# First Q ahead of K, V's first load behind its stores, and the last block's VectorE steps in source order

## The chip, the core and the metric

The kernel runs on one core of a Trainium2 chip. A core has five engines that run side by side and meet at semaphores: TensorE (PE in the profile, with PEld for its weight loads), VectorE (DVE), ScalarE (ACT), GpSimd (POOL) and SyncE (SP). Here SP does nothing but issue DMA transfers, in order: an issue that has to wait holds everything behind it. Each of the other engines works through its own instructions in order as well. The metric is the device time of one execution, in microseconds; lower is better.

## The reference

One transformer layer in float32 on x of shape (4, 2048, 256): attention with 16 heads of size 16 over 2048 keys, a layer norm, a gated feed-forward net of width 704 whose activations and weights are rounded blockwise (16 elements) to a 4-bit float grid, and a second layer norm.

```python
q, k, v = (split_heads(x @ W.T) for W in (Wq, Wk, Wv))      # 16 heads of 16
attn = softmax(einsum('bhld,bhmd->bhlm', q, k) / 4, axis=-1)
o = merge_heads(einsum('bhlm,bhmd->bhld', attn, v)) @ Wo.T
x = layernorm(x + o)
h = silu(fp4_linear(x, w_gate)) * fp4_linear(x, w_up)
x = layernorm(x + fp4_linear(h, w_down))                     # fp4_linear rounds both operands
```

## The kernel before

**Tiles and steps.** The queries are cut in blocks of 512 (`QB`), the keys in tiles of 128, the heads in four groups of four (`NG`, `HG`). A step is one group of heads for one query block: 4 x 4 x 4 = 64 steps of 16 key tiles. Each key tile is one period of the main loop (lines 860 to 898). In a period the maxima of a later key tile run ahead (`maxima`, 20 periods ahead: `LEAD`), the exponentials of the present one follow (`exponentials`), and two periods behind (`LAG`) the products with V (`values`). `period` fills each period with one or two parts of other work: projections of later blocks, the feed-forward net of finished ones, and the preparation of its weights (`prepare`).

**The start.** Lines 232 to 242 issue the first loads: x on SP's queue, the weights of K, Q and V on ScalarE's. `turn_w` transposes K's and then Q's weights. The loop at line 846 then projects the first 512 rows for K and Q, heads 0 to 7 ("k0", "q0"), and rows 512 to 2047 for K alone. `project` (line 333) transposes x, multiplies, splits each product into a high part (`hi`, ScalarE) and a rest (`lo`, GpSimd), and stores both to DRAM tensors `kx` and `qx`, four stores for each (line 362). `load_k` and `load_q` fetch them back per head: four transfers of 64 rows for K, four of 62 rows for Q. Only then can the first `maxima` run, which need both. V's projections are filled into the first 12 periods (m = 0 to 11 in the loop, n = m - 20); each stores to `vx` (line 378). V's first load is issued at n == 0 (line 867), in the period in which the exponentials begin.

**The end.** After the last period nothing but the last query block's own tail is left. `feed_forward_last` (line 678) does it in four tiles of 128 rows, t = 0 to 3, out of these pieces:

- `attended(t)`: output projection `py` on TensorE, added to x1 on VectorE (line 709), then `moments(t)`: two statistics steps on VectorE, two steps on GpSimd for the inverse deviation `rstd`;
- `quantized(t)`: normalises (line 699) and rounds to the 4-bit grid (`fp4_at_once`): 11 VectorE steps that each read the one before;
- `up(t)`: two transposes `ptq`, copied by ScalarE, then products `pg` and `pu`, read by ScalarE;
- `hidden(t)`: the gate's product and its rounding, 14 VectorE steps on 352 or 704 columns;
- `downward(t)`: transposes `pth`, copied by ScalarE, then the product `pz`;
- `added(t)` and `stored(t)`: adding `pz` (line 769), second layer norm, store to `out`.

**What sets the order.** A tile framework schedules what the source records. Matrix products are kept in the source's order (`matmul` and `transpose`, lines 134 to 138, call `keep_in_program_order`). For the other engines the framework picks among what it holds to be ready; in the last block it interleaves the VectorE steps of different tiles.

Of the kernel before, what the change touches and what calls it, by code (L numbers as in the profile page):

```python
# [35 lines left out]
ALU = mybir.AluOpType  # L36
# [34 lines left out]
    return 0 if j % 2 == 0 else DH  # L71


@with_exitstack
def block_kernel(
    ctx: ExitStack,
# [9 lines left out]
    out: bass.AP,  # L86
):
    nc = tc.nc
    B, L, D = x.shape
    FF = w_gate.shape[0]  # L90
    KC = D // P
    NQB = L // QB
# [75 lines left out]

    def fp4_at_once(pool, t, tag, gain=1.0):

        step = nc.vector
        p, nb, _ = t.shape
        amax = pool.tile([p, nb], F32, tag="amax" + tag, name="amax")
        step.tensor_reduce(amax, t, AX.X, ALU.max, apply_absolute_value=True)
        sc = pool.tile([p, nb], F32, tag="sc" + tag, name="sc")
        step.tensor_scalar(sc, amax, gain / 6.0, 1e-12, ALU.mult, ALU.max)
        rs = pool.tile([p, nb], F32, tag="rs" + tag, name="rs")
        step.reciprocal(rs, sc)
        step.tensor_scalar(rs, rs, gain * TIES_DOWN, 1.0, ALU.mult, ALU.mult)
        xn = pool.tile([p, nb, FB], F32, tag="xn" + tag, name="xn", bufs=3 if tag else 2)  # L180
        step.tensor_tensor(xn, t, rs.unsqueeze(2).to_broadcast([p, nb, FB]), ALU.mult)
        m = pool.tile([p, nb, FB], F32, tag="m" + tag, name="m", bufs=1)
        step.tensor_single_scalar(m.bitcast(I32), xn.bitcast(I32), EXPONENT, ALU.bitwise_and)
        step.tensor_scalar(m, m, 1.0, ROUND, ALU.max, ALU.mult)
        step.tensor_tensor(xn, xn, m, ALU.add)
        step.tensor_tensor(xn, xn, m, ALU.subtract)
        step.tensor_tensor(xn, xn, sc.unsqueeze(2).to_broadcast([p, nb, FB]), ALU.mult)
        return xn
# [27 lines left out]
    def load_x(b, tb):  # L216

        rows = slice(tb * QB, (tb + 1) * QB)
        if b == 0 and tb >= 2:
            xb_of[b, tb] = p1.tile([P, QT, D], F32, tag="x1", name="xb", bufs=2)  # L220
        else:
            xb_of[b, tb] = p2.tile([P, QT, D], F32, tag="xb", name="xb")
        nc.sync.dma_start(xb_of[b, tb], x[b, rows, :].rearrange("(t p) d -> p t d", p=P))
# [6 lines left out]
        nc.scalar.dma_start(loaded[name], w.rearrange("(c p) k -> p c k", p=P))  # L230

    load_x(0, 0)
    load_w("wk", wk)
    load_w("wq", wq)
    for tb in range(1, NQB):
        load_x(0, tb)
    ones = p2.tile([P, 2 * NC * L // P], F32, tag="a", name="ones")
# [6 lines left out]
    def turn_w(name, dst):  # L244
        for kc in range(KC):
# [7 lines left out]
            for n in range(KC):  # L253
# [2 lines left out]
                    pt[:, n * P : (n + 1) * P].rearrange("p (h d) -> p d h", h=NC),  # L256
                )

    turn_w("wk", wkT)
    turn_w("wq", wqT)  # L260


    RF = FF // 8
# [414 lines left out]
    def feed_forward_last(b, qb, x1):  # L678

        heads = [oTs[(b * NQB + qb) * KC + c] for c in range(KC)]  # L680
        xqT = p1.tile([P, KC, QB], F32, tag="xqT", name="xqT")
        xq, gates, hq, hT, norms = {}, {}, {}, {}, {}

        def wide(name):
            return p1.tile([P, QB], F32, tag="e", name=name, bufs=E_BUFS)

        def moments(t):
            st = p2.tile([P, 6], F32, tag="st", name="st")
            nc.vector.bn_stats(st, x1[:, t, :])
            mv = p2.tile([P, 4, 2], F32, tag="mv", name="mv")  # L690
            nc.vector.bn_aggr(mv[:, 0, :], st)
            rstd = p2.tile([P, 2], F32, tag="rstd", name="rstd")
            nc.gpsimd.tensor_scalar_add(rstd[:, :1], mv[:, 0, 1:2], LN_EPS)
            nc.gpsimd.tensor_tensor(rstd[:, :1], rstd[:, :1], minus_half[:, :1], ALU.pow)
            norms[t] = mv, rstd

        def normed(t):
            mv, rstd = norms.pop(t)
            nc.vector.tensor_scalar(
                x1[:, t, :], x1[:, t, :], mv[:, 0, 0:1], rstd[:, :1], ALU.subtract, ALU.mult  # L700
            )

        def attended(t):
            py = psum("py")
            for c in range(KC):
                matmul(
                    py[:, :D], heads[c][:, t * P : (t + 1) * P], woT[:, c, :], start=(c == 0), stop=(c == KC - 1)
                )
            nc.vector.tensor_add(x1[:, t, :], x1[:, t, :], py[:, :D])
            moments(t)  # L710

        def quantized(t):
            normed(t)
            xq[t] = fp4_at_once(p2, x1[:, t].rearrange("p (b f) -> p b f", f=FB), "")

        def up(t):
            pt = psum("ptq")[:, : KC * P].rearrange("p (k n) -> p k n", k=KC)
            for kc in range(KC):
                transpose(pt[:, kc, :], xq[t].rearrange("p b f -> p (b f)")[:, kc * P : (kc + 1) * P], ident)
            nc.scalar.copy(xqT[:, :, t * P : (t + 1) * P], pt)  # L720
            gates[t] = []
            for half in range(2):
                cols = slice(half * FH, (half + 1) * FH)
                pg, pu = psum("pg"), psum("pu")
                for bank, w in ((pg, wgT), (pu, wuT)):
                    for kc in range(KC):
                        matmul(
                            bank[:, :FH],
                            xqT[:, kc, t * P : (t + 1) * P],
                            w[:, kc, cols],  # L730
                            start=(kc == 0),
                            stop=(kc == KC - 1),
                        )
                a, g, u = (wide(name)[:, :FH] for name in "agu")
                nc.scalar.activation(a, pg[:, :FH], AF.Tanh, scale=0.5)
                nc.scalar.copy(g, pg[:, :FH])
                nc.scalar.copy(u, pu[:, :FH])
                gates[t].append((a, g, u))

        def hidden(t):  # L740
            h = p2.tile([P, FF], F32, tag="h", name="h")
            for half, (a, g, u) in enumerate(gates.pop(t)):
                nc.vector.scalar_tensor_tensor(a, a, 1.0, g, ALU.add, ALU.mult)
                nc.vector.tensor_mul(h[:, half * FH : (half + 1) * FH], a, u)
            hq[t] = fp4_at_once(p2, h.rearrange("p (b f) -> p b f", f=FB), "h", gain=0.5)

        def downward(t):
            if t % 2 == 0:
                hT[t // 2] = p2.tile([P, 2, NFC, P], F32, tag="hT", name="hT", bufs=1)
            q, dst = hq[t].rearrange("p b f -> p (b f)"), hT[t // 2][:, t % 2]  # L750
            for c0 in range(0, NFC, 4):
                pt = psum("pth")
                for c in range(c0, min(c0 + 4, NFC)):
                    w = min(P, FF - c * P)
                    transpose(pt[:w, (c - c0) * P : (c - c0 + 1) * P], q[:, c * P : c * P + w], ident)
                if c0 == 0:
                    nc.scalar.copy(dst[:, :4, :].rearrange("p c n -> p (c n)"), pt)  # L757
                    continue
                for c in range(c0, NFC):
                    w = min(P, FF - c * P)  # L760
                    nc.scalar.copy(dst[:w, c, :], pt[:w, (c - c0) * P : (c - c0 + 1) * P])
            pz = psum("pz")
            for c in range(NFC):
                w = min(P, FF - c * P)
                matmul(pz[:, :D], dst[:w, c, :], wdT[:w, c, :], start=(c == 0), stop=(c == NFC - 1))
            return pz

        def added(t, pz):
            nc.vector.tensor_add(x1[:, t, :], x1[:, t, :], pz[:, :D])
            moments(t)  # L770

        def stored(t):
            normed(t)
            at = qb * QB + t * P
            nc.sync.dma_start(out[b, at : at + P, :], x1[:, t, :])

        attended(0)
        attended(1)
        quantized(0)
        up(0)  # L780
        attended(2)
        quantized(1)
        up(1)
        hidden(0)
        attended(3)
        quantized(2)
        pz = downward(0)
        up(2)
        hidden(1)
        added(0, pz)  # L790
        quantized(3)
        pz = downward(1)
        up(3)
        hidden(2)
        stored(0)
        added(1, pz)
        pz = downward(2)
        hidden(3)
        stored(1)
        added(2, pz)  # L800
        pz = downward(3)
        stored(2)
        added(3, pz)
        stored(3)
# [39 lines left out]


    for tb in range(NQB):
        for _ in projection(0, tb, ("k0", "q0") if tb == 0 else ("k0",)):
            pass
        load_k(0, tb)
        if tb == 0:  # L850
            load_q(0)
    turn_w("wv", wvT)
    for tb in range(NQB):
        queue.append(projection(0, tb, ("v",)))
# [5 lines left out]
    for n in range(-LEAD, N + LAG):  # L860
        m = n + LEAD
        (sm, im), (s, kt), (sv, kv) = divmod(m, NKT), divmod(n, NKT), divmod(n - LAG, NKT)
        if m in (8, 10, 12, 14):
            if m == 8:
                load_q(1)
            load_k(1, m // 2 - 4)
        if n == 0:
            load_v(0)
        if n == N - NKT:
            x1_last = load_last(*steps[-1][:2])  # L870
# [64 lines left out]
```

## Time and profile before

| What | Value |
|---|---|
| median of 3 runs | 3654.88 us (3651.22 to 3658.14) |
| the profiled execution, as timed | 3651.45 us |
| its span, from first to last instruction | 3649.4 us |
| TensorE busy | 3534.1 us, 97% of the span |
| VectorE, ScalarE, GpSimd busy | 77%, 74%, 34% |
| mean granted TensorE clock | 0.989 |
| first score product | 27.40 us |
| first product with V | 99.19 us |
| last product with V, then the last block's tail | ends at 3572.1 us; the tail takes some 77 us |

The profile gives for each instruction its start, its duration, its source line and shape, and in square brackets how long its engine had stood idle before it and what ended that wait. A "chain" line tells on which engine the time that set the end was spent. In the rows of SP the duration is that of issuing a transfer, not of the transfer. TensorE is busy nearly all of the span; the exceptions lie in the first slice and the last one of the forty into which the page cuts the span.

### The profile page before, as it was taken

What the parts mean: (1) busy time and instruction counts of PE and PEld (TensorE: products, weight loads), DVE (VectorE), ACT (ScalarE), POOL (GpSimd) and SP (SyncE); (2) the same over time, 40 slices, a digit from 0 to 9 for tenths busy, and PEclk for the clock granted to TensorE, in tenths of its full rate; (3) what the DMA queues carried; (4) which work ended last, traced back from release to release, by engine and by line L of the source; (5) the groups of instructions that cost most, each with busy time, mean ns of one, the idle gap of its engine ahead of it and who ended that gap; (6) DMA issues with size and microseconds to landing.
All of it is one profiled execution on the core that took longest, in us unless ns stands there. A gap on an engine that the chain in (4) does not pass through costs nothing.

```text
span 3649.4 us, 57772 instructions
## 1 busy us (share of the span) xinstructions
PE 3534.1 (97%) x21348; PEld 1593.8 (44%) x21348; DVE 2816.2 (77%) x3310; ACT 2691.0 (74%) x5446; POOL 1251.3 (34%) x1496
## 2 busy tenths in 40 slices
PE   7889999999999999999999999999999999999996
PEld 5333444444444444444444444444443434444343
DVE  5777778787787778778787787878778787888845
ACT  3677777777777777777777777777777777777772
POOL 1331423434243242424324243342424325142430
PEclk9999999999999999999999999999999999999998
DMA  6533323323232322323223232322322221222100
GB/s 219 164 123 99 119 68 113 89 85 103 82 98 87 105 84 83 116 68 116 85 85 106 80 100 86 97 85 83 109 69 77 67 84 50 86 66 81 57 21 6
DMA packets 190640, 328.39 MB, mean 90 GB/s; under 512 B 24344, under 2 KB 68248, under 8 KB 190360
## 3 DMA queue, kind: packets, MB, share of 16 engines
q1 hardware_dynamic: 188968, 323.39, 29.1%
q8 instruction: 171, 2.80, 0.3%
q10 hardware_dynamic: 1392, 1.31, 0.1%
q14 instruction: 109, 0.89, 0.1%
HBM read 237.04 MB, written 86.51 MB: 89 GB/s over the span
## 4 chain that ended last, share of the span: by engine, by line
PE 82%; DVE 12%; DMA 2%; POOL 2%; issue 1%; ACT 1%; SPq 0%; POOLq 0%; ACTq 0%; DVEq 0%
PE av L135 24%; PE pe L135 18%; PE pm L135 16%; DVE mx L432 9%; PE pz L135 6%; PE pg L135 5%; PE pu L135 5%; PE pq L135 3%; PE pv L135 2%; PE pth L138 1%; PE pa L138 1%; PE py L135 1%; PE pn L138 1%; DMA qx<-qhi 1%; DVE st L524 1%
## 5 line engine op out<-in xcount | busy, mean ns | idle before, releaser
L432 DVE TENSOR_REDUCE mx<-pm 128x2 f32<-128x1024 f32 x2048 | 2408.6, 1217 | 666.5 <-PE pm L135 662.2
L466 ACT ACTIVATE e<-pe 128x512 f32<-128x512 f32 x4096 | 2218.8, 596 | 676.0 <-PE pe L135 670.8
L135 PE MATMUL av<-e,v 128*32 128x512 f32 x8192 | 1098.0, 608 | 4.2 <-DMA v<-vx 4.2
L135 PE MATMUL pe<-q,k 64*128 64x512 f32 x4096 | 1036.4, 456 | 4.9 <-ACT e L466 4.5
L135 PEld LDWEIGHTS pe<-q,k 64*128 64x128 f32 x4096 | 476.6, 184 | 968.5 <-ACT e L466 853.8
L135 PE MATMUL pm<-k,q 62*128 62x512 f32 x4096 | 805.1, 448 | 67.1 <-DVE mx L432 57.5
L135 PEld LDWEIGHTS pm<-k,q 62*128 62x128 f32 x4096 | 346.8, 185 | 382.7 <-DVE mx L432 178.2
L135 PEld LDWEIGHTS av<-e,v 128*32 128x32 f32 x8192 | 162.1, 108 | 335.5 <-issue 312.9
L572 POOL TENSOR_TENSOR a<-a,g 128x352 f32<-128x352 f32 x120 | 112.6, 938 | 494.5 <-ACT a L571 494.5
L135 PE MATMUL pz<-wdT,hT 128*128 128x128 f32 (+1 forms) x1488 | 233.4, 299 | 1.5 <-ACT hT L757 1.5
L617 POOL TENSOR_TENSOR x<-x,read 128x128 f32<-128x128 f32 x120 | 54.8, 456 | 482.2 <-ACT read L143 482.2
L135 PEld LDWEIGHTS pz<-wdT,hT 128*128 128x128 f32 x1488 | 190.5, 193 | 50.5 <-ACT e L466 18.2
L163 POOL TENSOR_TENSOR xn<-xn,m 128x704 f32<-128x704 f32 (+2 forms) x100 | 153.6, 1536 | 153.5 <-DVE m L162 131.6
L586 POOL TENSOR_TENSOR h<-a,u 128x352 f32<-128x352 f32 x120 | 112.4, 937 | 226.0 <-ACT u L585 224.0
L135 PE MATMUL pg<-wgT,xqT 128*128 128x352 f32 x512 | 186.5, 487 | 1.9 <-ACT xqT L720 1.9
L135 PE MATMUL pu<-wuT,xqT 128*128 128x352 f32 x512 | 185.0, 484 | 0.0
L548 POOL TENSOR_TENSOR x<-x,read 128x256 f32<-128x256 f32 x60 | 43.8, 730 | 374.0 <-ACT read L143 374.0
L164 POOL TENSOR_TENSOR xn<-xn,m 128x704 f32<-128x704 f32 (+2 forms) x100 | 153.8, 1538 | 5.4
L165 POOL TENSOR_TENSOR xn<-xn,sc 128x704 f32<-128x704 f32 (+2 forms) x100 | 126.4, 1264 | 7.5
L573 POOL TENSOR_TENSOR a<-a,g 128x352 f32<-128x352 f32 x120 | 113.9, 949 | 9.4
L135 PEld LDWEIGHTS pg<-wgT,xqT 128*128 128x128 f32 x512 | 87.5, 190 | 60.2 <-ACT e L466 19.1
L135 PEld LDWEIGHTS pu<-wuT,xqT 128*128 128x128 f32 x512 | 87.6, 189 | 58.1 <-ACT e L466 20.0
(114 smaller groups left out, 2278.8 us busy)
## 6 DMA issues: line engine op xcount, KB each, us to landing
k<-kx SPq DMA_DIRECT2D x1024, 128.0 KB
v<-vx SPq DMA_DIRECT2D x64, 768.0 KB
q<-qx SPq DMA_DIRECT2D x256, 124.0 KB
kx<-khi SPq DMA_DIRECT2D x64, 256.0 KB
qx<-qhi SPq DMA_DIRECT2D x64, 256.0 KB
vx<-vt SPq DMA_DIRECT2D x32, 384.0 KB
xb<-in_L_attn_x_dram SPq DMA_DIRECT2D x16, 512.0 KB
kx<-klo SPq DMA_DIRECT2D x32, 256.0 KB
```

Source lines behind the costliest of these rows:

```text
L135: tc.keep_in_program_order(nc.tensor.matmul(*args, **kw))
L138: tc.keep_in_program_order(nc.tensor.transpose(*args))
L163: nc.gpsimd.tensor_tensor(xn, xn, m, ALU.add)
L164: nc.gpsimd.tensor_tensor(xn, xn, m, ALU.subtract)
L165: nc.gpsimd.tensor_tensor(xn, xn, sc.unsqueeze(2).to_broadcast([p, nb, FB]), ALU.mult)
L432: nc.vector.tensor_reduce(mx_sb[s][:, t, 2 * i : 2 * i + 2, kb], pm, AX.X, ALU.max)
L466: nc.scalar.activation(e, pe[j], AF.Exp, scale=SCALE)
L548: nc.gpsimd.tensor_add(x1[:, t, :], x1[:, t, :], read(py[:, :D]))
L572: nc.gpsimd.tensor_mul(a, a, g)
L573: nc.gpsimd.tensor_add(a, a, g)
L586: nc.gpsimd.tensor_mul(h[:, cols], a, u)
L617: nc.gpsimd.tensor_add(x1[:, t, cols], x1[:, t, cols], read(pz))
```

## The change

Three things change.

1. At the start Q goes before K: its weights are loaded and transposed first, the first projection makes Q before K (so Q's four stores are issued before K's), and `load_q(0)` stands before `load_k(0, 0)`.
2. V's first load is no longer tied to n == 0. It is issued in the first period in which all of V's projections are recorded, which is m = 12 (n = -8).
3. In the last block VectorE's steps go through a wrapper, `InOrder`, that keeps them in the source's order; and `hidden(0)` is moved behind `attended(3)` and `quantized(2)`.

```diff
+class InOrder:
+    def __init__(self, tc, engine):
+        self.tc, self.engine = tc, engine
+
+    def __getattr__(self, name):
+        return lambda *args, **kw: self.tc.keep_in_program_order(getattr(self.engine, name)(*args, **kw))
...
+    vector = InOrder(tc, nc.vector)
...
     load_x(0, 0)
+    load_w("wq", wq)
     load_w("wk", wk)
-    load_w("wq", wq)
...
+    turn_w("wq", wqT)
     turn_w("wk", wkT)
-    turn_w("wq", wqT)
...
-            nc.vector.tensor_add(x1[:, t, :], x1[:, t, :], py[:, :D])
+            vector.tensor_add(x1[:, t, :], x1[:, t, :], py[:, :D])
...
         attended(2)
         quantized(1)
         up(1)
-        hidden(0)
         attended(3)
         quantized(2)
+        hidden(0)
         pz = downward(0)
         up(2)
         hidden(1)
...
-        for _ in projection(0, tb, ("k0", "q0") if tb == 0 else ("k0",)):
+        for _ in projection(0, tb, ("q0", "k0") if tb == 0 else ("k0",)):
             pass
-        load_k(0, tb)
         if tb == 0:
             load_q(0)
+        load_k(0, tb)
...
-        if n == 0:
+        if 0 not in v_sb and all((0, tb, "v") in projected for tb in range(NQB)):
             load_v(0)
```

The other replacements of `nc.vector` by `vector` are of the same kind: in `fp4_at_once`, `moments`, `normed`, `hidden` and `added`, which the last block alone uses.

In the two built programs every engine's instructions stand in the same order but for four places. Q and K are swapped at the start on all engines. SP's queue has V's first load among the K loads of the second step, four K loads after the last `vx` store and ahead of K's stores for heads 8 to 15. On VectorE the first reduction of `prepare` (`amax` on `wl`, line 150) stands one `mx` reduction later. And VectorE's last block runs in this order, where before the steps of neighbouring pieces alternated:

```
after:  add0 add1 | norm0+round0 | add2 | norm1+round1 | add3 | norm2+round2
        | hidden0 | hidden1 | added0 | norm3+round3 | hidden2
        | norm(stored0) added1 | hidden3 | norm(stored1) added2
        | norm(stored2) added3 | norm(stored3)
before: round0 and round1 alternate, ahead of add2; hidden0 alternates with
        add2, norm2+round2 and hidden1; hidden1 with added0 and round3; and so on
```

TensorE's order in the last block is the same in both: `py0 py1 ptq0 up(0) py2 ptq1 up(1) py3 pth0 pz0 ptq2 up(2) pth1 pz1 ptq3 up(3) pth2 pz2 pth3 pz3`.

More of the change, by code (lines that the diff above doesn't have):

```diff
@@ L169, in fp4_at_once @@
     def fp4_at_once(pool, t, tag, gain=1.0):
-        step = nc.vector
+        step = vector
         p, nb, _ = t.shape
@@ L688, in moments @@
             st = p2.tile([P, 6], F32, tag="st", name="st")
-            nc.vector.bn_stats(st, x1[:, t, :])
+            vector.bn_stats(st, x1[:, t, :])
             mv = p2.tile([P, 4, 2], F32, tag="mv", name="mv")
-            nc.vector.bn_aggr(mv[:, 0, :], st)
+            vector.bn_aggr(mv[:, 0, :], st)
             rstd = p2.tile([P, 2], F32, tag="rstd", name="rstd")
@@ L698, in normed @@
             mv, rstd = norms.pop(t)
-            nc.vector.tensor_scalar(
+            vector.tensor_scalar(
                 x1[:, t, :], x1[:, t, :], mv[:, 0, 0:1], rstd[:, :1], ALU.subtract, ALU.mult
@@ L742, in hidden @@
             for half, (a, g, u) in enumerate(gates.pop(t)):
-                nc.vector.scalar_tensor_tensor(a, a, 1.0, g, ALU.add, ALU.mult)
-                nc.vector.tensor_mul(h[:, half * FH : (half + 1) * FH], a, u)
+                vector.scalar_tensor_tensor(a, a, 1.0, g, ALU.add, ALU.mult)
+                vector.tensor_mul(h[:, half * FH : (half + 1) * FH], a, u)
             hq[t] = fp4_at_once(p2, h.rearrange("p (b f) -> p b f", f=FB), "h", gain=0.5)
@@ L768, in added @@
         def added(t, pz):
-            nc.vector.tensor_add(x1[:, t, :], x1[:, t, :], pz[:, :D])
+            vector.tensor_add(x1[:, t, :], x1[:, t, :], pz[:, :D])
             moments(t)
```

## The prediction

> **What bounds the kernel now.** I read the page first, for where time can be gained at all: its head and the slices.
>
> ```profile
> span 3649.4 us, 57772 instructions
> PE 3534.1 (97%) x21348; PEld 1593.8 (44%) x21348; DVE 2816.2 (77%) x3310; ACT 2691.0 (74%) x5446; POOL 1251.3 (34%) x1496
> PE   7889999999999999999999999999999999999996
> ```
>
> TensorE is the bound from the fourth slice to the 39th, and none of that is touched: there both programs have the same order on every engine. So the change can only matter in the first 300 us and in the last 77. I went through these two stretches in the timeline, engine by engine. TensorE and VectorE in the last block (start, duration, what; in brackets idle time and its releaser):
>
> ```profile
> 3582.93 0.42 DVE L185 TENSOR_TENSOR xn<-xn,m 128x256 f32<-128x256 f32 x1
> 3583.39 0.43 DVE L186 TENSOR_TENSOR xn<-xn,m 128x256 f32<-128x256 f32 x1
> 3583.85 0.43 DVE L187 TENSOR_TENSOR xn<-xn,sc 128x256 f32<-128x256 f32 x1
> 3584.33 0.69 PE L138 MATMUL ptq<-ident,xn 128*128 128x128 f32 x2 [7.08 <-DVE xn L187]
> 3585.48 2.72 PE L135 MATMUL pg<-wgT,xqT 128*128 128x352 f32 x4 [0.46 <-ACT xqT L720]
> 3591.70 1.03 PE L135 MATMUL py<-woT,oT 128*128 128x256 f32 x4
> 3592.56 0.38 PE L138 MATMUL ptq<-ident,xn 128*128 128x128 f32 x2
> 3593.40 1.45 PE L135 MATMUL pg<-wgT,xqT 128*128 128x352 f32 x4 [0.46 <-ACT xqT L720]
> 3602.53 1.51 PE L138 MATMUL pth<-ident,xn 128*128 128x128 f32 x6 [3.27 <-DVE xn L187]
> 3609.59 0.42 DVE L769 TENSOR_TENSOR x<-x,pz 128x256 f32<-128x256 f32 x1 [2.98 <-PE pz L135]
> 3634.10 0.42 DVE L769 TENSOR_TENSOR x<-x,pz 128x256 f32<-128x256 f32 x1 [1.81 <-PE pz L135]
> 3637.43 1.54 PE L138 MATMUL pth<-ident,xn 128*128 128x128 f32 x6 [3.37 <-DVE xn L187]
> ```
>
> The reader is to see three things. VectorE and TensorE take turns here, so each wait is on the path. At 3592.56 TensorE takes up tile 1 with no wait, right behind `py` of tile 2 (3591.70), since tile 1 was rounded on VectorE while TensorE did up(0). And a product after a long idle time is dear: the first `pg` took 2.72 us against 1.45 later; in that window the granted clock was 0.75.
>
> At the start:
>
> ```profile
> 27.40 0.18 PEld L135 LDWEIGHTS pm<-k,q 62*128 62x128 f32 x1 [2.79 <-DMA q<-qx]
> 34.81 0.28 PEld L135 LDWEIGHTS pm<-k,q 62*128 62x128 f32 x1 [2.23 <-DMA q<-qx]
> 99.19 1.32 PE L135 MATMUL av<-e,v 128*32 128x512 f32 x8 [4.17 <-DMA v<-vx]
> 117.32 0.68 DVE L150 TENSOR_REDUCE amax<-wl 88x32 f32<-88x512 f32 x1 [3.23 <-DMA wl<-in_L_ffn_w_gate_dram]
> 119.19 0.50 PE L135 MATMUL pm<-k,q 62*128 62x512 f32 x2 [2.79 <-DVE mx L432]
> ```
>
> TensorE waits for Q's four tiles one by one, then 4.17 us for V, then 2.79 us for VectorE, which itself waits for a weight.
>
> **The end, step by step.** First two durations. Rounding one tile of 256 columns: rows of .41, .42, .17, .24, .18, .42, .29, .29, .42, .43, .43 sum to 3.70; each step reads the one before, and 0.04 lies between such steps (3582.93 + 0.42 to 3583.39), ten times: **4.1 us**. hidden: .52, .53, .44, .53, then .88, .18, .42, .18, .89, .52, .52 and three of .89 are 8.28, with thirteen gaps **8.8 us**. An add with its two statistics (.42, .43, .17 and gaps) is 1.15.
>
> Steps that don't depend on each other start 0.33 us apart for the same 0.42 (3600.03 to 3600.36 in the timeline, likewise 0.80 for 0.89), so alternating tiles saves 0.13 a step. [...]
>
> 1. Tile 0 alone: its statistics no longer stand behind tile 1's add, 0.28 earlier, so it is normalised at 3578.53 instead of 3578.81; plus 4.1 it is done at 3582.6. `ptq0` comes at 3582.65, 1.7 us earlier. That is the gain.
> 2. ptq0 to the end of py2 takes 3592.73 - 3584.33 = 8.4 on TensorE: 3591.05. Now add2 waits for py2, and tile 1's rounding is queued **behind add2**. 1.15 + 4.1 later it is 3596.3; ptq1 started at 3592.56. TensorE stands idle 5.2 us where it had no wait.
> 3. up(1) and py3 take 3592.56 to 3599.27, 6.7, plus 1.3 for the cold clock (2.72 against 1.45): 3604.3.
> 4. add3 and tile 2's rounding, 5.25: 3609.55. Only now hidden(0), which before alternated with all this: 8.8, 3618.35. `pth0` before: 3602.53. It is **15.8 us late**.
> 5. TensorE from pth0 through up(2) took 3602.53 to 3615.38, cold clock included, 12.85: 3631.2. hidden(1) is done by 3627.2, so pth1 waits for nothing; 15.2 late (3616.00).
> 6. pth1 through up(3), 3616.00 to 3626.22, 10.2: 3641.4. VectorE meanwhile does added0, tile 3's rounding (3632.5, in time for ptq3 at 3635.5) and hidden(2): 3641.3. pth2 at 3641.4 against 3628.03, 13.4 late: the waits of 2.98 and 1.81 for `pz` that stood inside a hidden chain are gone.
> 7. One norm and added1, 1.4, then hidden(3), 8.8: 3651.5 against 3637.43, 14.1 late. From there to the end nothing changes.
>
> The end costs **+14.1**. Its bounds come from the clock, which I counted as cold in steps 2, 5 and 7: `pz` took 5.25 behind an idle time and 3.05 without, 2.2 us, and one and a half such amounts either way give +11 to +17.
>
> **The start.** *Q first.* Weights, transposes and projections swap like for like: two loads of 256 KB, two products. In SP's queue Q's four stores pass K's four, and Q's four loads pass K's four; K's loads, issued from 18.41, now stand where Q's stood, from 22.04. So Q can land at most 3.6 us earlier, 31.2 for the last. But K's four loads come behind it, 2.6 us of issue (18.41 to 21.04), which puts the last input at 33.8, or at 36.0 (34.81 + 1.2) if they queue behind Q's slow ones. VectorE's third reduction (38.27, idle 1.40 before it) is the first that would feel it. Bounds -3.6 and +1.2, taken -1.5. Q's tiles of 62 rows arrive 2.5 us apart (27.40 to 34.81 in three steps) in a stretch whose DMA share is 0.40. [...]
>
> *V.* The 4.17 us at 99.19 go. SP must wait for the last V store, issued at 73.6; K's last store (15.21) let its load go 3.2 us later (18.41), so V goes at about 77, some 0.3 us late, with four K loads and the stores for heads 8 to 15 behind it. Its 768 KB, 2.4 us at the 323 GB/s of 90 to 100 us, then fall into a stretch that is 0.90 to 0.92 busy (75 to 85). There GpSimd waits 9.95 us for such a store to free its buffer (86.19), ScalarE 1.07 for GpSimd (86.95), and the first exponentials follow with 0.63 of slack: up to 1.8 of it comes back. Bounds -4.2 and 0, taken -2.
>
> *amax one place later.* A reduction that TensorE needs no longer waits behind the weight: between -2.8 and 0, taken -1. Against all this stands that the chain of waits runs through transfers again later (11.13 us on `qx` from 160.24, 3.72 on `wl` from 171.45): where the queue sets the pace, time won before is lost. +1.5, at most all that was won.
>
> The start sums to **-3**, bounds -10.6 and +1.2.
>
> **Sum.** +14.1 - 3 = +11.1. On the profiled execution, 3651.45 (its span and 2.05 around it), that gives 3662.6. The median of the runs shown is 3.4 above it; on that it is 3666. I say 3665.
>
> **Rivals.** *The start pays for the end.* V, Q and amax all come through: -9 against +14, 3660 on the median. For: each wait is in the rows. Against: the busy queue. It decides if the first exponentials start 3 us earlier or more. Chance 0.22.
>
> *The end gains.* VectorE in order drops the waits of 2.98 and 1.81 for `pz` and the first 1.7: -6.5, with the start's -3 it is 3645 on the median. Place: the first turn of tile 1. It decides if tile 1's rounding still runs during up(0); then step 2's 5.2 us and what hangs on it don't come. Against it stands the built order, in which add2 precedes that rounding and `py2` follows up(0). Chance 0.04.
>
> *It doesn't do what it says:* V's early load holds SP until its stores land, and the K loads behind it are late. K's loads of that period are for key tiles that the maxima reach 14 periods on, so it costs at most what V gives: 3668, inside the forecast's range.
>
> **Chances.** Forecast 0.74, its own range 3660 to 3674. With the first rival's nearer part the range is 3656 to 3674. The runs shown spread by 0.19%, so 0.2%, 7.3 us, is about what can be told from no change. Slower by more: 0.73; within: 0.23; faster: 0.04.
>
> **What would show it.** In the profile after: idle TensorE of about 5 us before the second `ptq` and of 10 to 14 before the first `pth`, both released by DVE xn; `pth0` some 16 us after py3; no wait for v at the first `av`. It is wrong if the second `ptq` follows py2 without a wait, or if the span up to the last `av` shrinks by over 7 us.

## The result, and the profile after

The changed kernel took 3667.41 us (median of 6 runs, 3665.31 to 3672.31), the kernel before 3654.54 us on the same chip (6 runs, 3651.22 to 3658.14). The ratio is 1.0037 with a 95% interval of 1.0024 to 1.0050: slower by 9 to 18 us, more than the 0.2% that can be told from no change. The profiled execution took 3667.78 us, its span 3665.7 us, at a mean granted clock of 0.986 (before 0.989).

The head and the slices of the page say where:

```profile
span 3665.7 us, 57777 instructions
PE 3538.3 (97%) x21348; PEld 1597.3 (44%) x21348; DVE 2822.9 (77%) x3310; ACT 2690.1 (73%) x5446; POOL 1247.5 (34%) x1496
PE   7889999999999999999999999999999999999995
```

The slices are those of before but for the last, 5 tenths instead of 6. To cut the 16.3 us that the span grew by, I take one instant late in the main loop, the start of the last product with V: 3571.6 us before, 3572.4 after. So 0.8 us of it was there before the last block, and the last block itself took 93.35 us instead of 77.88, **15.5 us more**. The 0.8 is of these two executions only: in the profiles of four runs below whose program is that of before up to the last block, the last product with V starts at 3572.9 to 3581.9.

The last block in the timeline of the changed kernel (start, duration, what; in brackets idle time and its releaser). VectorE's rows all stand at line 81 now, which is the wrapper's:

```profile
3583.48 0.69 PE L149 MATMUL ptq<-ident,xn 128*128 128x128 f32 x2 [5.40 <-DVE xn L81]
3584.63 2.72 PE L146 MATMUL pg<-wgT,xqT 128*128 128x352 f32 x4 [0.46 <-ACT xqT L731]
3592.33 1.03 PE L146 MATMUL py<-woT,oT 128*128 128x256 f32 x4
3593.39 0.42 DVE L81 TENSOR_TENSOR x<-x,py 128x256 f32<-128x256 f32 x1 [9.96 <-PE py L146]
3598.59 0.66 PE L149 MATMUL ptq<-ident,xn 128*128 128x128 f32 x2 [5.24 <-DVE xn L81]
3599.72 2.71 PE L146 MATMUL pg<-wgT,xqT 128*128 128x352 f32 x4 [0.46 <-ACT xqT L731]
3606.70 1.03 PE L146 MATMUL py<-woT,oT 128*128 128x256 f32 x4
3607.76 0.42 DVE L81 TENSOR_TENSOR x<-x,py 128x256 f32<-128x256 f32 x1 [9.32 <-PE py L146]
3621.75 1.51 PE L149 MATMUL pth<-ident,xn 128*128 128x128 f32 x6 [14.02 <-DVE xn L81]
```

Read the two engines against each other. VectorE stands idle for 9.96 and 9.32 us in front of the two adds, waiting for `py`. Each time TensorE stands idle right afterwards, 5.24 and 14.02 us, waiting for the rounding (and the second time also for `hidden(0)`) that is queued behind that add. While one works the other waits. Before, the second `ptq` had no wait at all, and the first `pth` 3.27 us.

The start:

```profile
35.00 1.78 PE L146 MATMUL pm<-k,q 62*128 62x512 f32 x4 [9.11 <-DMA k<-kx]
91.60 2.09 PE L146 MATMUL pe<-q,k 64*128 64x512 f32 x4 [1.14 <-DMA q<-nr]
119.81 0.68 DVE L161 TENSOR_REDUCE amax<-wl 88x32 f32<-88x512 f32 x1 [3.69 <-DMA wl<-in_L_ffn_w_gate_dram]
122.22 0.59 PE L146 MATMUL pm<-k,q 62*128 62x512 f32 x2 [3.03 <-DVE mx L443]
```

The four first score products no longer wait for Q's tiles one by one (27.40 to 34.81 before); all four now wait for K, until 35.00. The wait of 4.17 us for V is gone from the first `av`, but the first `pe` now waits 1.14 us for Q's last two rows (`q<-nr`), and the wait behind VectorE's wait for the first weight is still there, 3.03 us where it was 2.79. The first `av` itself comes no earlier, at 101.30 instead of 99.19; why is told with `v_only` below.

### The profile page after: what moved, and what is told of

It reads as the page before. It is cut to its first block, busy times and chain, and to the rows that moved or that the text cites. A ratio compares the mean times of both kernels' runs of the same rounds, so it can differ in the third digit from the quotient of the medians.

```text
span 3665.7 us, 57777 instructions
## 1 busy us (share of the span) xinstructions
PE 3538.3 (97%) x21348; PEld 1597.3 (44%) x21348; DVE 2822.9 (77%) x3310; ACT 2690.1 (73%) x5446; POOL 1247.5 (34%) x1496
## 4 chain that ended last, share of the span: by engine, by line
PE 82%; DVE 13%; DMA 2%; POOL 1%; issue 1%; ACT 1%; SPq 0%; POOLq 0%; ACTq 0%; DVEq 0%
PE av L146 24%; PE pe L146 18%; PE pm L146 16%; DVE mx L443 8%; PE pz L146 5%; PE pg L146 5%; PE pu L146 5%; PE pq L146 3%; PE pv L146 2%; PE pth L149 1%; PE pa L149 1%; PE py L146 1%; PE pn L149 1%; DMA qx<-qhi 1%; DVE xn L81 1%
```

## The experiments

A time by itself is the median, a ratio is to the kernel before on the same chip, with its 95% interval. A difference in us is the ratio times the time of before.

### The end alone, and the start alone

`end_only` is the kernel before with part 3 (the wrapper on VectorE, and `hidden(0)` moved); `start_only` has parts 1 and 2 and the old last block.

```diff
# end_only, against before
+    vector = InOrder(tc, nc.vector)
...
-        hidden(0)
         attended(3)
         quantized(2)
+        hidden(0)
# start_only, against after
-    vector = InOrder(tc, nc.vector)
...
+        hidden(0)
         attended(3)
         quantized(2)
-        hidden(0)
```

> The kernel before with part 3 alone: VectorE of the last block in the source's order and hidden(0) behind quantized(2); weights, Q, K and V as before. Theory (the last block costs everything and the start gives nothing back): about +15 us, with idle TensorE of about 5 us before the second ptq and 13 to 15 before the first pth. Rival (the start's part lost several us that the main loop hides from the milestones, so that the end cost less than the two traces make it): +10 us or less.

> Parts 1 and 2 alone: Q first, and V's first load early; the last block as before. Theory: TensorE is about 2 us later at the first 600 us and about 1 us later at the end of the main loop, so +1 us, within 0 to +2. Rival (the prediction's sum): -3 us. The first maximum is to come 5 to 6 us later than before (30.60), and the wait for v at the first av is to be gone, with a wait for q<-nr before the first pe in its place.

`end_only`: 3669.46 us, ratio 1.0041 (1.0028 to 1.0053), which is +15 us (10 to 19). `start_only`: 3652.75 us, ratio 0.9995 (0.9986 to 1.0004), -2 us (-5 to +1.5). The end costs everything. In the trace of `end_only` the last block takes 91.77 us, 13.9 more than before; the changed kernel, with the same block, had 15.5 more, so single executions of it differ by 1.6 us. The start's part can't be told from nothing, and this run alone doesn't part its theory (+1) from its rival (-3). The wait for `q<-nr` that was expected ahead of the first `pe` isn't in its trace; the first `av` comes at 96.7 us.

### Which half of part 3 costs it

`end_no_move` keeps the wrapper and leaves `hidden(0)` where it was; `end_move_only` moves `hidden(0)` and leaves the order to the scheduler.

```diff
# end_no_move, against end_only
         up(1)
+        hidden(0)
         attended(3)
         quantized(2)
-        hidden(0)
# end_move_only, against before
         up(1)
-        hidden(0)
         attended(3)
         quantized(2)
+        hidden(0)
```

> VectorE of the last block in the source's order, but hidden(0) left where it was, right behind up(1); the start as before. Theory (of the end's loss, the most is hidden(0) standing behind add 3 and the rounding of tile 2, about 5.3 us, and what is late behind it; the rest is the first turn of tile 1 and the chains that run one by one): +6 us, pth0 some 3 us later than before instead of 19, no long idle time before it. Rival (the place of hidden(0) costs nothing, the order as such costs all): +15 us, as with both.

> hidden(0) moved behind quantized(2) in the source, but VectorE's order still left to the scheduler; the start as before. Theory (the scheduler still mixes hidden(0)'s steps with add 3's and with the rounding of tile 2): +1 us, within -1 and +3, the second ptq without a wait. Rival (the place alone costs hidden(0) its turn): +8 us or more, with idle TensorE of over 8 us before the first pth.

`end_no_move`: 3662.56 us, ratio 1.0021 (1.0012 to 1.0030), +8 us (4 to 11). `end_move_only`: 3654.33 us, ratio 1.0000 (0.9991 to 1.0009). TensorE in the last block of `end_no_move`:

```profile
3593.38 1.03 PE L146 MATMUL py<-woT,oT 128*128 128x256 f32 x4
3599.63 0.66 PE L149 MATMUL ptq<-ident,xn 128*128 128x128 f32 x2 [5.23 <-DVE xn L81]
3607.46 1.03 PE L146 MATMUL py<-woT,oT 128*128 128x256 f32 x4
3608.42 0.85 PE L149 MATMUL pth<-ident,xn 128*128 128x128 f32 x6
3613.62 0.44 PE L149 MATMUL ptq<-ident,xn 128*128 128x128 f32 x2 [0.85 <-DVE xn L81]
```

The first turn is as in the changed kernel, 5.23 us of idle TensorE behind add2. But `pth` follows the fourth `py` without a wait: `hidden(0)` ran on VectorE during up(1). So the 15 us split into about 7.7 for the fixed order with its first turn, and 7.3 for `hidden(0)` behind add3 and round2, each uncertain by 4 us or more by the times; the last blocks of the traces, 84.54 us here and 91.77 in `end_only`, make it 6.7 and 7.2. The move by itself costs nothing that the times show, where the scheduler orders VectorE: in the trace of `end_move_only` the second `ptq` has no wait and the first `pth` waits 4.69 us instead of 3.27. It is dear only together with the wrapper.

### Q and V one by one, and the rows of Q

Four kernels, each with one profiled execution and so without an interval:

```diff
# q_only, against before: part 1. v_only, against before: part 2.
# q_split, against before; q_first_split, against q_only
             for j in range(2):
-                nc.sync.dma_start(
-                    q[R * j : R * j + RM, :].bitcast(F32), qx[(b * NQB + qb) % len(qx)][c][:RM, h + j, :]
-                )
+                for r0, r1 in ((0, 48), (48, RM)) if s == 0 else ((0, RM),):
+                    nc.sync.dma_start(
+                        q[R * j + r0 : R * j + r1, :].bitcast(F32), qx[(b * NQB + qb) % len(qx)][c][r0:r1, h + j, :]
+                    )
```

> The kernel before with Q first alone; V's load and the last block as before. [...] Rival (the prediction: the loads only change places): the first maximum at 31 to 34, nothing lost or a gain of 1.5 us. V's wait of 4.17 us at the first av stays.

> The kernel before with V's first load early alone. Theory (the wait for v goes, and one for q<-nr ahead of the first pe comes in its place, 1 to 2 us, with a clock of 0.5 behind it): first av at 96 to 98 us, against 99.2 to 102.9 in four runs that load V as before; the four K loads of this stretch are issued some 3 us later, and nothing waits for them. Rival (V's load takes as much from the stores of the same stretch as it saves): first av at 99 or later.

> Q first alone, with each of the first step's four Q loads of 62 rows cut into one of 48 rows and one of 14; nothing else changed. [...] Rival (K is late because it is issued behind Q, whatever the engines): the first maximum at 33 or later.

> The kernel before with the same cut of the first step's Q loads into 48 and 14 rows; K first as before. Theory: Q's tiles no longer land 2.5 us apart; the first maximum at 28 to 29 instead of 30.6, the second 1.2 us behind it instead of 5, the 40th reduction 3 to 5 us earlier. Rival (the tiles land 2.5 us apart for another reason, such as the time between issues): the second maximum still about 5 us behind the first.

| us from the span's start | before | q_only | v_only | q_first_split | q_split |
|---|---|---|---|---|---|
| first `mx` reduction | 30.6 | 35.1 | 31.1 | 26.4 | 25.8 |
| second | 35.6 | 36.3 | 36.1 | 27.9 | 27.7 |
| 41st | 88.2 | 89.7 | 88.7 | 80.7 | 80.7 |
| first `av` | 99.2 | 102.4 | 96.8 | 93.3 | 93.7 |
| 161st `mx` | 316.9 | 323.2 | 320.9 | 313.6 | 313.6 |
| time as run | 3657.76 | 3657.74 | 3655.55 | 3647.99 | 3645.10 |

The times of before come from its profile shown above, except the last row, which is its run beside these four. In four more profiles whose start up to V's load is that of before, the 41st reduction lay at 88.8 to 90.5 us; so differences of 2 us in that row say nothing, and 8 us do. In the row of the 161st these four profiles spread from 317.1 to 326.7, so it says little.

*Q first gained nothing in these traces*, since the products then wait for K (9.12 us, until 33.95, in `q_only`). The cut points to the cause: it brought the first reduction to 26 us in either order, where 28 to 29 was expected of `q_split`, and the 41st forward by some 8 us. Here is the busy share of the DMA engines from 18 to 36 us, in 40 slices of 0.45 us, of the changed kernel:

```profile
DMA  9999997201111111167767993112941118811129
DMA packets 1619, 2.92 MB, mean 162 GB/s; under 512 B 192, under 2 KB 192, under 8 KB 1619
```

and of `q_first_split`, whose queue has the same order but for the cut:

```profile
DMA  9998874636442758678989999999995176676998
DMA packets 2583, 4.43 MB, mean 246 GB/s; under 512 B 426, under 2 KB 426, under 8 KB 2582
```

In the first row there are stretches of ones: from 22.1 to 25.7 us, when Q's four loads are out (a DMA share of 0.13, 44 GB/s), and again, with bursts between, from 29 to 35 (0.34 with the bursts), when K's are still missing at TensorE, though issued from 23.36 on. In the second row a single one is left, 4.43 MB move in the time of 2.92, and the longest wait of the first four score products for K is 0.36 us instead of 9.11. So in these stretches most of the DMA engines' time went unused while loads were due, and with the cut more of it was used. How many engines a load of 62, 48 or 14 rows uses is not shown by the DMA share; that the gain comes from the sizes of the pieces is my reading, not a measurement. A cut into pieces of other sizes was not run, so that eight transfers in flight instead of four are what helped isn't excluded by a run; against it stands that four loads in flight together took no more than 0.13 of the engines' time there.

*V early is given back.* In `v_only` TensorE waits:

```profile
90.42 0.81 PE L135 MATMUL pe<-q,k 64*128 64x512 f32 x3 [1.02 <-DMA q<-nr]
119.66 0.80 PE L135 MATMUL pm<-k,q 62*128 62x512 f32 x2 [5.35 <-DVE mx L432]
```

The first `av` comes at 96.8 instead of 99.2 or later, as the theory had it, and then the wait at 119 us is 5.35 us instead of 2.79. VectorE waits there for the first weight of `prepare`, 6.01 us instead of 3.23. That weight was issued earlier (107.69 instead of 109.88), but was used at the same time (117.25 and 117.32): this transfer sets the pace, and it did not come earlier. What the first `av` won is gone by then. (`start_only` shows the same: first `av` early, then 7.04 us.) More profiles bear it out: with Q's loads uncut the weight was first used at 117.3 to 120.5 us in the six that load V late, and at 117.2 to 119.8 in the three that load it early. Why the transfer took longer is not shown.

The changed kernel itself lost V's gain sooner. Its rows, and those of `start_only`, which has the same start:

```profile
97.72 2.07 PE L146 MATMUL pq<-xT,wkT 128*128 128x256 f32 x4
101.30 1.39 PE L146 MATMUL av<-e,v 128*32 128x512 f32 x8
```

```profile
94.76 1.13 PE L135 MATMUL pq<-xT,wkT 128*128 128x256 f32 x4
96.71 1.07 PE L135 MATMUL av<-e,v 128*32 128x512 f32 x8
```

From 92 to 102 us its granted clock was 0.50, and the four products `pq` of the first row took 2.07 us, where they took 1.13 in `start_only` and in `v_only`. `v_only` had nearly the same wait for `q<-nr` before it, 1.02 us, so that wait alone doesn't bring such long products.

### An order by hand, and both gains together

`hand` changes the last block, with the start of before. It keeps the wrapper, and writes VectorE's order out so that, where it can be had, no step that waits for TensorE stands ahead of one that TensorE waits for, and so that two chains of dependent steps alternate wherever there are two. The chains became generators; `both` takes one step of each in turn, `late(n, ..)` lets n turns pass first, and `through(t)` is `hidden(t)` with `downward(t)` behind it. TensorE's order changes with it (all four `py` first, up(2) ahead of the first `pth`), and `g`, `u`, `m`, `mv` and `rstd` get more or other buffers (not shown below). None of these was tried by itself.

```diff
+        py = [product(t) for t in range(2)]
+        both(sums(0, py[0]))
+        both(sums(1, py[1]))
+        py += [product(t) for t in range(2, 4)]
+        both(quantized(0))
         up(0)
-        attended(2)
-        quantized(1)
+        both(quantized(1), after(sums(2, py[2]), sums(3, py[3])))
         up(1)
-        hidden(0)
-        attended(3)
-        quantized(2)
-        pz = downward(0)
+        both(quantized(2))
         up(2)
...
+        both(through(0), quantized(3))
         up(3)
...
+        both(
+            through(1),
+            late(5, lambda: through(2)),
+            late(10, lambda: through(3)),
+            late(9, lambda: sums(0, pz[0])),
+            late(26, lambda: stored(0), lambda: sums(1, pz[1])),
+        )
```

> The kernel before with the first step's four Q loads cut into 48 and 14 rows, timed (the same program as in the look before). Theory (the cut brings the first 40 reductions forward by 8 us, and no later wait gives it back): -8 to -12 us. Rival (the later waits for weights give most of it back, as they did with V's load): -3 us or less.

> The last block alone, VectorE in an order written out by hand: all four products of woT first, tile 0's rounding alone, every later chain of dependent steps alternating with a second one, up(2) ahead of pth0, the adds of pz behind the steps that TensorE waits for; the tiles g and u in K's freed buffers and two buffers for m, so that nothing waits for a free one. The start as before. Theory (VectorE in the source's order is dear only where the source puts a step that waits for TensorE, or a long chain that nobody waits for yet, ahead of one that TensorE waits for): -12 us, -9 to -14, no idle TensorE of over 5 us between the first ptq and the third pth. Rival (an order fixed by hand is itself dear, since it can't follow the real times): 0 or slower.

> Both: the cut Q loads and the last block in the order by hand. Theory (start and end are 3400 us apart and add up): -20 to -24 us. Rival (one of them is given back): -12 us or less.

| kernel | median us | ratio (95%) | difference |
|---|---|---|---|
| q_split_5 | 3646.43 | 0.9976 (0.9967 to 0.9985) | -9 us (-5 to -12) |
| hand | 3642.50 | 0.9964 (0.9951 to 0.9978) | -13 us (-8 to -18) |
| hand_q_split | 3633.87 | 0.9943 (0.9930 to 0.9955) | -21 us (-16 to -26) |

All three lie in the ranges of their theories, and the two gains add up within their intervals. TensorE in the last block of `hand`:

```profile
3581.56 3.29 PE L146 MATMUL py<-woT,oT 128*128 128x256 f32 x14 [0.24 <-ACT oT L525]
3588.53 0.69 PE L149 MATMUL ptq<-ident,xn 128*128 128x128 f32 x2 [3.68 <-DVE xn L81]
3596.72 0.38 PE L149 MATMUL ptq<-ident,xn 128*128 128x128 f32 x2
3602.54 0.38 PE L149 MATMUL ptq<-ident,xn 128*128 128x128 f32 x2
3608.36 0.82 PE L149 MATMUL pth<-ident,xn 128*128 128x128 f32 x6
3620.51 0.87 PE L149 MATMUL pth<-ident,xn 128*128 128x128 f32 x6 [1.96 <-DVE xn L81]
3626.35 0.88 PE L149 MATMUL pth<-ident,xn 128*128 128x128 f32 x6
```

Between the first `ptq` and the third `pth` one wait of TensorE for VectorE is left, 1.96 us, and the block takes 63.9 us from the last `av`'s start, against 77.88 before and 93.35 after the change. A fixed order is not dear in itself; how much of the gain is VectorE's order, TensorE's or the buffers is not parted.

### V early on top of these

`all_v` adds part 2 to `hand_q_split`.

```diff
-        if n == 0:
+        if 0 not in v_sb and all((0, tb, "v") in projected for tb in range(NQB)):
             load_v(0)
```

> The cut Q loads and the last block by hand, and V's first load early besides. Theory (VectorE's wait for the first weight, some 20 us after the first av, takes back what the wait for v gives): the same as without V's early load, 3634 us within 2, first av 2 to 4 us earlier (92.2 before), the wait for mx behind it longer by about as much. Rival (V's wait was a loss of its own): 3630 us or less.

Ratio to before 0.9946 (0.9933 to 0.9960), by which it takes some 3635 us, against 0.9943 without it: nothing that can be told, as the theory had it. The first `av` comes at 90.8 instead of 92.2, somewhat less than the 2 to 4 us expected, and the waits for `mx` around 112 us are 3.48 and 1.69 instead of 1.41 and 1.64.

## Why the prediction was right, and where it was not

3665 us, slower, 3656 to 3674 was said; 3667.4 came, 12.9 above the median of before where the sum had 11.1. The end made it so, by the steps named; its +14.1 was 1.4 too small in this profile, and near in that of `end_only` (13.9). The start's terms were wrong one by one, but their sum of -3 is too small a thing for the times to tell: `start_only` has -2, between -5 and +1.5. That the total came so near is in this part luck.

*Step 1* (the gain of 1.7 us at tile 0): the first `ptq` came at 3583.48, which is 0.85 earlier than before, with a block that began 0.83 later: 1.7. Right.

*Step 2* had py2 end 8.4 us after `ptq0` and then 5.2 us of idle TensorE. The idle time was 5.24. The stretch before it took 9.9 (3583.48 to 3593.36): 1.5 too small. *Step 3* took up(1) and py3 as 6.7 + 1.3 = 8.0; they took 9.1 (3598.59 to 3607.73), 1.1 too small. Both are the same term, the clock: in step 2 I had taken the stretch as long as before, and in step 3 I had priced a cold start by one `pg` (2.72 against 1.45). By the granted clock in the stretches, after and before the change:

```profile
3583.50:3593.40 9.90, 9.39 (x22) 5.52 (x22) 0.01 (x1) 2.89 (x7) 0.00 (x0) 0.65 0.00 0
3598.60:3607.70 9.10, 8.64 (x22) 5.08 (x22) 0.00 (x0) 2.10 (x5) 0.00 (x0) 0.70 0.00 0
```

```profile
3584.30:3592.70 8.40, 7.91 (x24) 5.08 (x24) 3.58 (x9) 2.90 (x7) 0.00 (x0) 0.76 0.00 0
3592.70:3599.30 6.60, 6.10 (x23) 3.72 (x20) 5.95 (x19) 2.90 (x7) 0.78 (x2) 1.00 0.00 1
```

(The columns are the stretch and its length, busy time and instructions of PE, PEld, DVE, ACT and POOL, then the granted clock, the DMA share and GB/s.) up(0) ran at 0.65 instead of 0.76 and up(1) at 0.70 instead of 1.00: the low clock reached past `pg` into `pu` (2.55 and 2.27 us, against 1.35 in up(1) of before, at 1.00). The bounds of +11 to +17 allowed for this term, and 15.5 lies in them. The size is of one execution: in `end_only` the same two stretches took 8.98 and 8.69 us, 0.6 and 0.7 more than the sum had.

*Step 4* (add3, rounding and hidden(0) in a row, 5.25 + 8.8 = 14.05 us from the end of py3 to `pth0`): 3607.73 to 3621.75, 14.0. Right, so the gaps between dependent steps were well taken from the rows, and `end_no_move` shows that this place is about half of the loss.

*Steps 5 and 6* (12.85 and 10.2 us from one `pth` to the next): 12.67 and 10.0. Right, no wait ahead of either. *Step 7*: `pth3` came 16.8 late instead of 14.1: 0.8 is the block's later start, the rest what steps 2 and 3 had left; from there to the end 0.5 was made good.

*Q first, -1.5 taken, bounds -3.6 and +1.2.* The value was the wrong one of the two. K did queue behind Q; the case "36.0 if they queue behind Q's slow ones" is what came (35.00 for the products, the third reduction at 39.45 instead of 38.27, the bound of +1.2). The profile had the sign of it, Q's tiles 2.5 us apart at a low DMA share (the 0.40 given for it is the share from 30 to 40 us; from 27.40 to 34.81 it was 0.57, with stretches of 0.13 and 0.16 in it); I still took a value between the bounds.

*V, -2 taken, bounds -4.2 and 0.* The wait went, as said, and the times show no gain from it, the other end of the range. The step that failed is how much "comes back". I looked for it at 75 to 87 us in the stores; some of it is there (the 1.14 us for `q<-nr`). In `v_only` and `start_only` the most came back at 119 us, in the wait for the first weight, and in the changed kernel's own profile before the first `av`, at a granted clock of 0.50. The prediction had the first only in its +1.5 below, and the second not at all.

*amax, -1 taken.* One place later shows no gain: the wait is 3.03 us instead of 2.79. But VectorE's own wait for this weight is 0.69 to 3.23 us in the profiles with the start of before, so the size of this term stays open. *+1.5, given back where the queue sets the pace*, was the right mechanism at the wrong size: as far as the times tell it took all of it, which the prediction had as its limit.

How large the start's part is stays open within -5 to +1.5 us, by `start_only`; the pair of profiles says +0.8, but the same start differs by several us from one execution to the next.

*The rivals.* "The start pays for the end" fell by its own sign: the first `pe`, which the first exponentials read, came at 91.60 us instead of 88.69, later and not 3 us earlier. "The end gains" would have needed tile 1's rounding during up(0). In `hand` the second `ptq` does follow without a wait, with much else changed, and there the block takes 14 us less than before. "V's load holds SP" came in part: no wait for K appears, but three of the four kernels with V early wait 1.0 to 1.2 us for `q<-nr` ahead of the first `pe`, the ten others 0.2 us at most.

## What to carry to other kernels

When an order by hand replaces a scheduler's, look on each in-order engine for a step that waits for another engine and see what is queued behind it: here two adds of 0.42 us, put ahead of what TensorE needed next, were followed by 5 and 14 us of idle TensorE. A wait that is removed early in a pipeline is worth only what the next wait on the same input stream doesn't take: look for the transfer that sets the pace before counting the gain. And where transfers come in one by one at a low DMA share, look at how they are cut before their order: here cutting 62 rows into 48 and 14 brought 9 us, and no reordering of the loads brought anything that could be told.

## What the runs showed of the hardware

- Four loads of 62 rows (124 KB each) reached TensorE about 2.5 us apart (27.40, 29.77, 32.30 and 34.81 us), and in stretches of this time the DMA share was 0.13 to 0.16; cut into 48 and 14 rows, the first two reductions came at 25.8 and 27.7 us instead of 30.6 and 35.6. The DMA share shows how much of the engines' time was used, not by which of them.
- What an idle time costs the products behind it was not one number. In the last block of before the `pz` behind the first `pth`, which had waited 3.27 us, took 5.25 us, at a granted clock of 0.76 from 3602.50 to 3615.40; in `start_only`, with the same order and a wait of 3.26 us, it took 3.92; behind the second `pth`, after waits of 0.62 and 0.61 us, it took 3.05 in both. From the `py` rows at 3575.68 and 3579.82 to the end the two blocks took 73.7 and 71.5 us. What sets the amount is not shown by these runs.
- A VectorE step of 0.42 us that reads the one before it started 0.46 us after it (3582.93 to 3583.39 before), one that doesn't 0.33 us (3600.03 to 3600.36), so two alternating chains take less time than one after the other. VectorE was busy 52.16 us of the 63 us from 3577 to 3640 in `hand`, 48.94 of 69 (3577 to 3646) before.
